# A third buffer for result tiles behind the y phase, and a later place for layer 1's third unit, in a two-layer graph kernel

## The chip, the cores and the metric

The kernel runs on one core of a Trainium2 chip. The metric is the time of one execution on the device in microseconds (us), and lower is better. The engines of a core work side by side, each through its own list of instructions in order: PE (TensorE, matrix products), DVE (VectorE), ACT (ScalarE), POOL (GpSimd, which here issues nearly all gathers and scatters) and SP (SyncE, which issues the plain transfers). An instruction that waits for another engine or for a transfer holds back everything behind it on its own engine.

## The reference, cut to what matters

A graph of 2708 nodes with 1024 features each, and two layers. Layer 0 is attention over the neighbours of a node, layer 1 a sum over the neighbours. Each is followed by a residual and a layer norm.

```python
# layer 0
q = x @ W_q.T + b_q;  k = x @ W_k.T + b_k;  v = x @ W_v.T + b_v
z = (q @ k.T) / sqrt(1024) * adj
z = where(z == 0, -10000, z)
x = layernorm(x + relu(softmax(z, axis=1) @ v))
# layer 1
x = layernorm(x + adj @ (x @ weight) + bias)
```

The matrix `adj` holds zeros and ones and is nearly empty, so the kernel works with lists of neighbours.

## The kernel before

**Blocks.** The rows are sorted by their number of neighbours and cut into 22 blocks of 128 rows. Block 0 holds the rows with most neighbours, block 21 (the list `last`) is the short one of 20 rows without any. `SLOTS` gives the neighbours that a block can have.

**The stages.** First the weights of q and k are multiplied into one matrix, and the lists of neighbours are made from `adj`. Then the y phase computes a row of scores' factors per row of x (`y_block`, L319 to L328), block by block, and stores it in DRAM. Beside it, and behind it, "jobs" attend: they gather y rows (`yg`) and neighbours' rows (`g`), take scores on DVE (L774), and sum the neighbours' rows with the weights of the softmax into a tile `r` (L831). A finished `r` is transposed by PE (L698) and copied to SBUF by ACT (L699).

**The projections of layer 0.** Until the y phase is over, blocks are projected one at a time: `project` (L721), then `finish0`, which adds the bias into a tile `t` (L867), applies relu and adds the row's own x (L869), normalises with `norm` (ACT at L757 to L770) and scatters the tile `t` to the DRAM tensor of layer 1's inputs (L685, called x_d in the profile). Blocks 1, 0 and 21 come last in this manner. Behind them seven pairs of blocks follow, (7, 20), (19, 18) and so on. A pair is one 2 by 2 block product in seven half products where eight would be the plain way (`pair_products`, products at L958). It needs sums and differences of the two transposed tiles (`turn_pair`, L947 to L950, tile `s_all`), and differences of the weights, made once on DVE (L1089 to L1092; the profile calls these tiles t as well). Between the products DVE adds partial results from PSUM into the two result tiles (`add`, L970), since only four PSUM banks serve the products. `finish_pair` (L1027) does for a pair what `finish0` does for a block.

**Where the result tiles lie.** Tiles named `t` come from two pools. The pool `work` (`wp`) has two buffers of `t`, used in turn: by every block of `finish0` and by the first tile of every pair. The pool `xb` exists only behind the y phase, in memory that the y phase used before; it has two buffers of `t`, for the second tile of every pair. A buffer is free again when the scatter of the tile before has landed. So the first tile of pair (7, 20) takes the buffer of block 0, and the first tile of pair (19, 18) that of block 21.

**Layer 1.** It runs over 11 units of one or two blocks, the first four being (20), (19, 18), (17, 16) and (15, 1). `sum_rows` gathers neighbours' rows on POOL and sums them on DVE (L1189, L1191). `turn1` transposes and takes sums and differences as above. `gather_x1` copies the bias into a tile `xr` on ACT (L1198), and a gather on POOL adds the rows' own x to it. `work1` makes the products, and `finish1` normalises and scatters to the output.

**What sets the order.** A scheduler orders each engine's instructions when the program is built. It goes by the order of the code, by priorities (the adds from PSUM are urgent) and by its own estimates. `follow` adds a dependency by hand; with `same=True` it is between two instructions of one engine and only fixes their order. In layer 1, the sums of the third unit, (17, 16), stand in the code ahead of the loop, thus ahead of the second unit's `turn1` and `gather_x1`.

Of the kernel before, what the change touches and what calls it, by code (L numbers as in the profile page):

```python
# [9 lines left out]
F32 = mybir.dt.float32  # L10
# [5 lines left out]
ALU = mybir.AluOpType  # L16
# [4 lines left out]
P = 128  # L21
# [59 lines left out]
def sparse_part(ctx, tc, x, xT, adj, wqT, wkT, wvT, bq, bk, bv, w1, b1, out):  # L81
    nc = tc.nc
    N, D = x.shape
# [15 lines left out]
    last = [b for b in range(NB) if SLOTS[b] == 0]  # L99
# [12 lines left out]
    with es:  # L112
# [146 lines left out]
        for c in range(DC):  # L259
            nc.vector.scalar_tensor_tensor(junk[:, :D], wq_i[c // 2][:, c % 2, :], scale, bk_bc, op0=ALU.mult,  # L260
                                           op1=ALU.mult, accum_out=u_col[:, c:c + 1])
        for c in range(DC):
            nc.vector.scalar_tensor_tensor(junk[:, D:2 * D], wk_i[:, c, :], 1.0, bq_bc, op0=ALU.mult,
                                           op1=ALU.mult, accum_out=y_col[:, c:c + 1])
        nc.vector.scalar_tensor_tensor(junk[:, :DC], bq_sb, scale, bk_sb, op0=ALU.mult,
                                       op1=ALU.mult, accum_out=bqk)
# [69 lines left out]
        def follow(later, earlier, same=False):  # L336

            kind = mybir.DependencyClass.NoSync if same else mybir.DependencyClass.Sync
            tc.add_manual_dep(later.ins, earlier.ins.name, mybir.DependencyInfo(kind, mybir.DependencyReason.DATA),
                              reason="an engine's queue shall not stand still for a transfer")  # L340
# [287 lines left out]
        for b in range(FAMILY):  # L628
# [8 lines left out]
            elif FAMILY - DC // 2 - 2 <= b < FAMILY - 2:  # L637
                for c in range(2 * (b - FAMILY + DC // 2 + 2), 2 * (b - FAMILY + DC // 2 + 2) + 2):
                    for h in range(NH):
                        put = nc.sync.dma_start(out=wv_q[c // 4][h][:, c % 4, :],  # L640
                                                in_=wvT[c * P:(c + 1) * P, h * HALF:(h + 1) * HALF])
# [14 lines left out]
        wp = es.enter_context(tc.tile_pool(name="work", bufs=2, reuse_waits="tile"))  # L656
# [27 lines left out]
        def scatter(dst, b, n, src, group):  # L684
            put = nc.gpsimd.indirect_dma_start(  # L685
                out=dst, out_offset=bass.IndirectOffsetOnAxis(ap=tabs[:n, b, ROW:ROW + 1], axis=0),
                in_=src[:n], in_offset=None)
            tc.declare_no_dep(put.ins, group=group, reason="disjoint rows: a row's number is in one record")
            tc.add_to_no_dep_group(group, put.ins)
# [59 lines left out]
        def norm(t, sm, n, sm2=None):  # L749

            nm = stat.tile([P, 1], F32, name="lnm")
            if sm2 is None:
                nc.vector.tensor_scalar_mul(nm[:n], sm[:n], -1.0 / D)
            else:
                nc.vector.tensor_scalar(nm[:n], sm[:n], sm2[:n], -1.0 / D, op0=ALU.add, op1=ALU.mult)  # L755
            vs = stat.tile([P, 1], F32, name="vs")
            nc.scalar.activation(junks[:n], t[:n], AF.Square, bias=nm[:n], accum_out=vs[:n])  # L757

            lv = stat.tile([P, 1], F32, name="lv")
            nc.scalar.activation(lv[:n], vs[:n], AF.Ln, bias=eps[:n], scale=1.0 / D)  # L760
            near = stat.tile([P, 1], F32, name="near")
            nc.scalar.activation(near[:n], lv[:n], AF.Exp, scale=-0.5)
            ve = stat.tile([P, 1], F32, name="ve")
            nc.vector.scalar_tensor_tensor(ve[:n], vs[:n], D * EPS, near[:n], op0=ALU.add, op1=ALU.mult)
            nc.vector.tensor_scalar(ve[:n], ve[:n], near[:n], -0.5 / D, op0=ALU.mult, op1=ALU.mult)
            rstd = stat.tile([P, 1], F32, name="rstd")
            nc.vector.scalar_tensor_tensor(rstd[:n], ve[:n], 1.5, near[:n], op0=ALU.add, op1=ALU.mult)
            nmr = stat.tile([P, 1], F32, name="nmr")
            end = nc.vector.tensor_tensor(nmr[:n], nm[:n], rstd[:n], op=ALU.mult)  # L769
            applied.append(nc.scalar.activation(t[:n], t[:n], AF.Identity, bias=nmr[:n], scale=rstd[:n]))  # L770
            return end
# [88 lines left out]

        def finish0(b, po, xr):
            n = rows[b]
            t = wp.tile([P, D], F32, name="t")
            for h in range(NH):
                hs = slice(h * HALF, (h + 1) * HALF)
                with tc.high_priority(URGENT):
                    nc.vector.tensor_add(t[:n, hs], po[h][:n], bias_bc[:n, hs])  # L867
            sm = stat.tile([P, 1], F32, name="sm")
            nc.vector.scalar_tensor_tensor(t[:n], t[:n], 0.0, xr[:n], op0=ALU.max, op1=ALU.add, accum_out=sm[:n])  # L869
            end = norm(t, sm, n)  # L870
            scatter(x1_d[:, :], b, n, t, "x1")
            return end
# [60 lines left out]
            yield  # L933


        def turn_pair(flips, pool):

            A = []
            for k, flip_to in enumerate(flips):
                rT = (pool if k else wp).tile([P, DC, P], F32, name="rT", bufs=2)  # L940
                A.append(flip_to(rT))
            if len(flips) == 1:
                return A, None
            (a11, a12), (a21, a22) = [(a[:, :DC // 2], a[:, DC // 2:]) for a in A]
            s_all = wm_pool.tile([P, 4, DC // 2, P], F32, name="s_all", tag="m3")
            S = [s_all[:, i] for i in range(4)]
            nc.vector.tensor_add(S[0], a21, a22)  # L947
            nc.vector.tensor_sub(S[1], S[0], a11)
            nc.vector.tensor_sub(S[2], a11, a21)
            nc.vector.tensor_sub(S[3], a12, S[1])  # L950
            return A, S

        def differences():
# [8 lines left out]
        def halves_of(t):  # L962
            return t[:, :HALF], t[:, HALF:]
# [4 lines left out]
        def add(to, acc, what):  # L968
            with tc.high_priority(URGENT):
                nc.vector.tensor_add(to, acc, what)  # L970
# [39 lines left out]
            return a[:, :DC // 2], a[:, DC // 2:]  # L1010

        def project_pair(pair, A, S):
            ts = [(xb_pools[0] if k else wp).tile([P, D], F32, name="t", bufs=2) for k in range(2)]
            bias = halves_of(bias_bc)

            def whole(k, h, acc, what):
                add(halves_of(ts[k])[h], acc, what)

            pair_products(A, S, wv_q, wv_t, [bias, bias], [halves_of(t) for t in ts], whole, pair == pairs[-1])
            return ts  # L1020
# [13 lines left out]
        got, xb_bc, xb_pools, pair_x = {}, [], [], {}  # L1034
# [137 lines left out]
        units = [(20,), (19, 18), (17, 16), (15, 1), (14, 2), (7, 8), (9, 3), (4, 10), (6, 0), (5, 11), (12, 13)]  # L1172
        assert sorted(last + [b for unit in units for b in unit]) == list(range(NB))
        last_norm = applied[-1]
        firsts = []

        def sum_rows(b, k=0):
            if b == "hub":
                n, tab, ok, r = P, tab_h, valid_h, part
            else:  # L1180
                n, tab, ok = (P, tab0, valid0) if b == 0 else (rows[b], tabs[:, b, :SLOTS[b]], valid[:, b, :SLOTS[b]])
                r = (cp if k else wp).tile([P, D], F32, name="r", bufs=RB)
            for j in range(tab.shape[1] if b else J0):
                if j == 0 and b not in [0, "hub"] + single + MIXED:
                    gather_slot(x1_d[:, :], tab[:n, 0:1], n, r)
                    continue
                xg = gather_slot(x1_d[:, :], tab[:n, j:j + 1], n, g_tile())
                if j == 0:
                    firsts.append(nc.vector.tensor_scalar(r[:n], xg[:n], ok[:n, 0:1], None, op0=ALU.mult))  # L1189
                else:  # L1190
                    nc.vector.scalar_tensor_tensor(r[:n], xg[:n], ok[:n, j:j + 1], r[:n], op0=ALU.mult, op1=ALU.add)  # L1191
            return r

        def gather_x1(b, k=0):

            n = rows[b]
            xr = (cp if k else wp).tile([P, D], F32, name="xr", bufs=2 if k else 3)
            follow(nc.scalar.copy(xr[:n], bias1[:n]), last_norm, same=True)  # L1198
            return gather_at(x1_d[:, :], tabs[:n, b, ROW:ROW + 1], n, xr, ALU.add)
# [40 lines left out]
        got1, turned1, pending = {}, {}, []  # L1240
# [5 lines left out]
        nc.vector.tensor_sub(t3, t2, w11)  # L1246
        nc.vector.tensor_sub(t4, w21, t2)
        xrs = {0: [gather_x1(b, k) for k, b in enumerate(units[0])]}
        got1[2] = [sum_rows(b, k) for k, b in enumerate(units[2])]
        for i, unit in enumerate(units):  # L1250
            for p in pending:
                finish1(*p)
            if i + 1 < len(units):
                turned1[i + 1] = turn1(units[i + 1], got1.pop(i + 1))
                xrs[i + 1] = [gather_x1(b, k) for k, b in enumerate(units[i + 1])]
            if i + 3 < len(units):
                got1[i + 3] = [sum_rows(b, k) for k, b in enumerate(units[i + 3])]
            if i == 4:
                sum_rows("hub")
            pending = list(zip(unit, *work1(unit, *turned1.pop(i), xrs.pop(i))))  # L1260
            if i == 2:
                for b in last:
                    pending.append((b, gather_x1(b), None))
# [319 lines left out]
```

## Time and profile before

| | |
|---|---|
| median of three runs | 1090.86 us (1090.35 to 1092.21) |
| span of the profiled execution | 1091.0 us |
| busy: PE, DVE, ACT, POOL | 1015.2, 826.3, 428.1, 486.7 us |
| PE's products of pairs and units (L958, three groups) | 126.6 + 87.9 + 72.1 us |
| mean granted clock of PE | 0.976 |

The span has four parts for the reader of this case: up to about 540 us the weights, the lists and the y phase; from 540 to 582 the last single blocks 1, 0 and 21; from 582 to 771 the seven pairs; and from 783 to the end layer 1. Between 770.7 and 783.1 PE has nothing to do, since layer 1 gathers rows that layer 0 has to write first. The names in the profile are those of the program without their numbers: `t<-po,bias_bc` at L970 is an `add` into a result tile, `x_d<-t,tabs` at L685 is a scatter of a result tile, `g<-in_x_dram,tabs` a gather of neighbours' rows in layer 0 and `g<-x_d,tabs` in layer 1.

### The profile page before, as it was taken

The numbers are of one execution on the slowest core, as the hardware profiler recorded it, in microseconds if no ns is written. First come the engines' busy times: TensorE is split into PE (matmuls) and PEld (weight loads), VectorE is DVE, ScalarE is ACT, GpSimd is POOL, SyncE is SP. The second block draws the span as 40 slices with busy tenths as digits, with TensorE's granted clock in tenths as the row PEclk, the third lists the DMA queues.
The fourth block names the chain that finished last, engine by engine and source line by source line (L and its number), as shares of the span: only waits on it lengthen the run. The fifth ranks groups of instructions, "written<-read, shape, count | busy, mean of one in ns | idle before, by whom it ended". The sixth has DMA issues, their size and how long they took to land.

```text
span 1091.0 us, 10751 instructions
## 1 busy us (share of the span) xinstructions
PE 1015.2 (93%) x3177; PEld 540.1 (50%) x3177; DVE 826.3 (76%) x1801; ACT 428.1 (39%) x896; POOL 486.7 (45%) x397
## 2 busy tenths in 40 slices
PE   7999999999798989999998999999589999999993
PEld 6444466556454545466644444444244444445441
DVE  8799999980487789965297999984477777896431
ACT  4688697412131323232333253342512363324322
POOL 1000230067453546623066476631477777887300
PEclk9999999999999999999999899999799999999997
DMA  9555468435786746635142487835598689979601
GB/s 363 193 211 202 164 219 292 137 95 153 259 261 209 236 160 222 212 126 187 43 124 97 140 275 261 280 125 183 159 302 245 207 241 320 297 221 321 180 39 41
DMA packets 85219, 218.22 MB, mean 200 GB/s; under 512 B 15354, under 2 KB 37338, under 8 KB 82444
## 3 DMA queue, kind: packets, MB, share of 16 engines
q0 software_dynamic: 48768, 148.05, 42.3%
q1 hardware_dynamic: 36384, 69.40, 18.8%
q8 instruction: 27, 0.44, 0.2%
q14 instruction: 40, 0.33, 0.1%
HBM read 208.60 MB, written 33.68 MB: 222 GB/s over the span
## 4 chain that ended last, share of the span: by engine, by line
DVE 32%; PE 28%; issue 18%; DMA 10%; POOL 7%; ACT 3%; POOLq 0%; DVEq 0%; ACTq 0%
PE po L958 17%; PE po L319 6%; DVE few L225 6%; DVE a L222 5%; DVE junkv L774 5%; DMA g<-in_x_dram,tabs 4%; DVE r L831 3%; PE po L721 2%; POOL g L349 2%; DVE t L970 1%; POOL tab_d L563 1%; DMA g<-x_d,tabs 1%; DMA yg<-y_d,tabs 1%; PE tr L247 1%; POOL xr L343 1%
## 5 line engine op out<-in xcount | busy, mean ns | idle before, releaser
L319 PE MATMUL po<-m_sb,xt 128*128 128x343 f32 (+1 forms) x1008 | 296.3, 454 | 11.5 <-DVE yo L323 6.3
L319 PEld LDWEIGHTS po<-m_sb,xt 128*128 128x128 f32 x1008 | 190.4, 190 | 111.9 <-DVE yo L323 8.0
L774 DVE SCALAR_TENSOR_TENSOR junkv<-yg,g 128x1024 uint8<-128x1024 f32 x109 | 133.1, 1221 | 28.5 <-DMA g<-in_x_dram,tabs 16.2
L349 POOL DMA_INDIRECT g<-in_x_dram,tabs x86 | 114.3, 1330 | 76.4 <-ACT r L829 25.2
L958 PE MATMUL po<-t,s_all 128*128 128x512 f32 x272 | 126.6, 609 | 10.6 <-DVE t L970 6.5
L1191 DVE SCALAR_TENSOR_TENSOR r<-g,valid,r 128x1024 f32<-128x1024 f32 x77 | 98.6, 1281 | 17.8 <-DMA g<-x_d,tabs 17.2
L608 PE MATMUL po<-wk_o,wq_o 128*128 128x512 f32 x256 | 110.5, 592 | 0.0
L721 PE MATMUL po<-wv,rT 128*128 128x512 f32 x224 | 101.7, 611 | 6.2 <-DVE yo L323 2.8
L757 ACT ACTIVATE junks<-t,lnm 128x1024 uint8<-128x1024 f32 (+1 forms) x43 | 49.3, 1147 | 120.8 <-DVE lnm L755 103.9
L332 ACT ACTIVATE junka<-xt 128x128 f32<-128x128 f32 x176 | 53.9, 307 | 100.7 <-PE po L319 62.1
L958 PEld LDWEIGHTS po<-t,s_all 128*128 128x128 f32 x272 | 52.6, 196 | 78.2 <-issue 61.1
L958 PE MATMUL po<-w,rT 128*128 128x512 f32 x192 | 87.9, 607 | 0.0
L349 POOL DMA_INDIRECT g<-x_d,tabs x67 | 77.0, 1149 | 22.7 <-issue 16.5
L831 DVE SCALAR_TENSOR_TENSOR r<-g,pr,r 128x1024 f32<-128x1024 f32 x64 | 82.0, 1281 | 6.3 <-ACT r L843 4.8
L563 POOL DMA_INDIRECT tab_d<-rec,pos_i x22 | 25.1, 1141 | 129.9 <-DVE pos_i L552 123.5
L770 ACT ACTIVATE t<-t,nmr,rstd 128x1024 f32<-128x1024 f32 (+1 forms) x43 | 52.5, 1237 | 70.7 <-DVE nmr L769 64.2
L225 DVE MAX8 few<-a 128x8 f32<-128x75 f32 (+3 forms) x132 | 78.8, 616 | 0.0
L608 PEld LDWEIGHTS po<-wk_o,wq_o 128*128 128x128 f32 x256 | 48.4, 190 | 59.3 <-issue 59.0
L721 PEld LDWEIGHTS po<-wv,rT 128*128 128x128 f32 x224 | 43.2, 195 | 60.0 <-issue 53.5
L958 PE MATMUL po<-w,s_all 128*128 128x512 f32 x160 | 72.1, 592 | 0.0
L222 DVE SCALAR_TENSOR_TENSOR a<-a,iota 128x2708 f32<-128x2708 f32 (+1 forms) x22 | 65.2, 2963 | 5.4 <-ACT junk L221 5.4
L220 ACT ACTIVATE junk<-a 128x2708 uint8<-128x2708 f32 (+1 forms) x22 | 54.1, 2458 | 26.9 <-DMA a<-in_adj_dram 22.3
(332 smaller groups left out, 1475.4 us busy)
## 6 DMA issues: line engine op xcount, KB each, us to landing
a<-in_adj_dram SPq DMA_DIRECT2D x21, 1354.0 KB, 5.7
y_d<-yo SPq DMA_DIRECT2D x21, 514.0 KB, 5.4
xt<-in_xT_dram SPq DMA_DIRECT2D x21, 512.0 KB, 5.6
wq_i<-in_wqT_dram SPq DMA_DIRECT2D x8, 512.0 KB, 10.0
wk_i<-in_wkT_dram SPq DMA_DIRECT2D x8, 512.0 KB, 10.2
wv<-in_wvT_dram SPq DMA_DIRECT2D x16, 256.0 KB, 6.8
w<-in_w_dram SPq DMA_DIRECT2D x4, 1024.0 KB, 6.5
g<-in_x_dram,tabs POOLq DMA_INDIRECT x86, 5.6
```

What stands on the lines that cost most here:

```text
L220: nc.scalar.activation(junk[:n], a[:n], AF.Sign, accum_out=cnt[:n, b:b + 1])
L222: nc.vector.scalar_tensor_tensor(a[:n], a[:n], 1.0, iota[:n], op0=ALU.is_equal, op1=ALU.mult)
L225: nc.vector.max(few[:n, i * 8:(i + 1) * 8], a[:n, cuts[i]:cuts[i + 1]])
L319: put = nc.tensor.matmul(po[:, :k1 - k0], xt[:, c, :], m_sb[c // 2][:, c % 2, k0:k1], start=(c == 0), stop=(c == DC - 1))
L332: put = nc.scalar.activation(junka, xts[b][:, c, :], AF.Copy, accum_out=xs[:, c, b:b + 1])
L349: nc.gpsimd.indirect_dma_start(out=dst[:n], out_offset=None, in_=src, in_offset=bass.IndirectOffsetOnAxis(ap=at, axis=0), bounds_check=N - ...
L608: nc.tensor.matmul(po, wq_o[i // 2][:, o, i % 2 * P:(i % 2 + 1) * P], wk_o[:, o, hs], start=(o == 0), stop=(o == DC - 1))
L721: put = nc.tensor.matmul(acc, rT[:, c, :], w[c // 4][h][:, c % 4, :], start=(c == 0), stop=(c == DC - 1))
L774: nc.vector.scalar_tensor_tensor(junkv[:n], yg[:n, :D], scale, xg[:n], op0=ALU.mult, op1=ALU.mult, accum_out=s)
L831: nc.vector.scalar_tensor_tensor(r[:n], xg[j][:n], pr[:n, j:j + 1], r[:n], op0=ALU.mult, op1=ALU.add)
L958: put = nc.tensor.matmul(acc, a[:, k], w[:, k], start=start and k == 0, stop=stop and k == DC // 2 - 1, skip_group_check=True)
L1191: nc.vector.scalar_tensor_tensor(r[:n], xg[:n], ok[:n, j:j + 1], r[:n], op0=ALU.mult, op1=ALU.add)
```

## The change

It has two parts. In the first, the result tiles of blocks 0 and 21 (`[0] + last`) come from the pool `xb`, whose `t` gets a third buffer. The pool `work` keeps two, so that the first tile of pair (7, 20) takes the buffer of block 2 or 1, which are further back. In the second, the sums of layer 1's third unit move in the code behind the second unit's `turn1` and `gather_x1`, and the first sum of each of its two blocks is ordered on DVE behind the last difference of the second unit (`halves_turned[-1]`).

```diff
         def finish0(b, po, xr):
             n = rows[b]
-            t = wp.tile([P, D], F32, name="t")
+            t = xb_pools[0].tile([P, D], F32, name="t", bufs=3) if b in [0] + last else wp.tile([P, D], F32, name="t")
...
         def turn_pair(flips, pool):
...
-            nc.vector.tensor_sub(S[3], a12, S[1])
+            halves_turned.append(nc.vector.tensor_sub(S[3], a12, S[1]))
...
         def project_pair(pair, A, S):
-            ts = [(xb_pools[0] if k else wp).tile([P, D], F32, name="t", bufs=2) for k in range(2)]
+            ts = [(xb_pools[0] if k else wp).tile([P, D], F32, name="t", bufs=2 + k) for k in range(2)]
...
-        def sum_rows(b, k=0):
+        def sum_rows(b, k=0, behind=None):
...
+                if behind is not None:
+                    follow(put, behind, same=True)
+                    behind = None
...
-        got1[2] = [sum_rows(b, k) for k, b in enumerate(units[2])]
         for i, unit in enumerate(units):
...
             if i + 1 < len(units):
                 turned1[i + 1] = turn1(units[i + 1], got1.pop(i + 1))
                 xrs[i + 1] = [gather_x1(b, k) for k, b in enumerate(units[i + 1])]
+            if i == 0:
+                got1[2] = [sum_rows(b, k, halves_turned[-1]) for k, b in enumerate(units[2])]
```

In the built program PE, ACT and SP issue what they issued before; PE's and ACT's order differs by neighbours that change places in layer 0. On DVE the adds of pair (7, 20) stand earlier, and the rest of layer 0 differs by small swaps; in layer 1 two sums of the third unit stand behind the four differences of the second. On POOL one gather of y rows late in layer 0 stands behind two gathers of `xr`, and in layer 1 the two `xr` gathers of the second unit stand ahead of the third unit's four gathers.

More of the change, by code (lines that the diff above doesn't have):

```diff
@@ L933, in attend_shares @@
             yield
+        halves_turned = []
         def turn_pair(flips, pool):
@@ L1188, in sum_rows @@
                 if j == 0:
-                    firsts.append(nc.vector.tensor_scalar(r[:n], xg[:n], ok[:n, 0:1], None, op0=ALU.mult))
-                else:
-                    nc.vector.scalar_tensor_tensor(r[:n], xg[:n], ok[:n, j:j + 1], r[:n], op0=ALU.mult, op1=ALU.add)
+                    put = nc.vector.tensor_scalar(r[:n], xg[:n], ok[:n, 0:1], None, op0=ALU.mult)
+                    firsts.append(put)
+                else:
+                    put = nc.vector.scalar_tensor_tensor(r[:n], xg[:n], ok[:n, j:j + 1], r[:n], op0=ALU.mult, op1=ALU.add)
+                if behind is not None:
+                    follow(put, behind, same=True)
+                    behind = None
             return r
```

## The prediction

> **What bounds the kernel now.** I read first the busy times of each engine in stretches that I cut at the idle times of PE (columns: stretch, its length, busy time of PE, PE weight loads, DVE, ACT and POOL with instruction counts, granted PE clock, DMA share, GB/s):
>
> ```profile
> 581.50:594.80 13.30, 13.25 (x38) 5.94 (x36) 12.21 (x20) 6.69 (x13) 11.77 (x2) 1.00 0.13 40
> 594.80:601.30 6.50, 0.04 (x1) 0.04 (x1) 0.79 (x2) 0.00 (x0) 2.94 (x3) 0.84 0.48 162
> 601.30:619.20 17.90, 17.90 (x42) 8.30 (x43) 16.56 (x38) 4.43 (x9) 8.83 (x7) 0.87 0.50 152
> 619.20:649.00 29.80, 29.80 (x83) 14.01 (x81) 29.65 (x63) 11.62 (x21) 20.40 (x15) 1.00 0.74 239
> 649.00:735.00 86.00, 84.89 (x240) 40.29 (x239) 82.46 (x202) 38.26 (x72) 47.61 (x39) 1.00 0.65 222
> 735.00:770.70 35.70, 35.68 (x85) 15.78 (x83) 15.60 (x43) 8.35 (x15) 3.58 (x4) 1.00 0.56 193
> ```
>
> PE runs without a stop to 594.8, stands 6.5 us, and then runs almost without a stop to 770.7. DVE stands in the same hole and is then as full as PE until about 730; after that it has room. So before the hole, inside it and after it nothing but this one stop is loose. The timeline of PE and of DVE at that place (start, length, instruction, idle time before it and what ended it), and POOL's:
>
> ```profile
> 592.87 1.88 PE L958 MATMUL po<-wv,rT 128*128 128x512 f32 x4
> 601.26 6.07 PE L958 MATMUL po<-t,s_all 128*128 128x512 f32 x8 [6.51 <-DVE t L970]
> 608.89 3.60 PE L958 MATMUL po<-t,s_all 128*128 128x512 f32 x8
> ```
>
> ```profile
> 592.44 1.26 DVE L831 SCALAR_TENSOR_TENSOR r<-g,pr,r 128x1024 f32<-128x1024 f32 x1
> 600.51 1.29 DVE L970 TENSOR_TENSOR t<-po,bias_bc 128x512 f32<-128x512 f32 x2 [6.81 <-DMA x_d<-t,tabs]
> 607.37 0.69 DVE L970 TENSOR_TENSOR t<-po,bias_bc 128x512 f32<-128x512 f32 x1 [1.07 <-PE po L958]
> ```
>
> ```profile
> 587.11 7.48 POOL L349 DMA_INDIRECT g<-in_x_dram,tabs  x1 [0.30 <-DVE rstd L767]
> 594.89 0.93 POOL L343 DMA_INDIRECT xr<-in_x_dram,tabs  x1 [0.30 <-issue]
> 596.13 1.00 POOL L685 DMA_INDIRECT x_d<-t,tabs  x1 [0.30 <-issue]
> ```
>
> The chain reads from the right: PE waits for a DVE add (the first of pair (7, 20)); DVE waits for the scatter of block 0's result, because the add writes the buffer of "t" that this scatter still reads; the scatter stands on POOL behind a gather that took 7.48 us. The result itself was ready at 589.25 (ACT's L770 began at 588.01 and took 1.24).
>
> The second place is the start of layer 1, PE and then DVE:
>
> ```profile
> 802.47 1.99 PE L698 MATMUL tr<-ident,r 128*128 128x128 f32 x16
> 804.29 7.03 PE L958 MATMUL po<-w,rT 128*128 128x512 f32 x16
> 814.87 5.09 PE L958 MATMUL po<-t,s_all 128*128 128x512 f32 x8 [3.54 <-DVE xr L970]
> ```
>
> ```profile
> 801.55 0.68 DVE L1222 SCALAR_TENSOR_TENSOR t<-po,xr 128x512 f32<-128x512 f32 x1
> 807.48 1.28 DVE L1191 SCALAR_TENSOR_TENSOR r<-g,valid,r 128x1024 f32<-128x1024 f32 x1 [5.24 <-DMA g<-x_d,tabs]
> 814.13 0.68 DVE L970 TENSOR_TENSOR xr<-po,xr 128x512 f32<-128x512 f32 x1
> ```
>
> PE stands 3.54 us for the add at 814.13, which DVE reaches only after sums that wait for the fourth unit's gathers.
>
> **What the Trainium skill says.** "TensorE: Matmul & The Clock Gate", section "What's actually happening": an idle window of about 3.4 us halves the clock until a busy window has passed. The trace agrees: the eight matmuls after the hole took 6.07, the same eight later 3.60. "SBUF — State Buffer", section "Who interferes with whom": a DVE instruction with two SBUF inputs blocks a GpSimd instruction that reads SBUF, for its whole length. The trace fits: the 7.48 us gather lay beside the two 2.27 us differences of weights (L1091, L1092), while the gathers of 560 to 625 have a median of 1.22. "Advanced Engine Details and Errata", section "Sequencer Loop": an instruction waits in its engine's queue until its semaphore is ready. Here DVE issues nothing for 6.81 us, so all behind the add waits too.
>
> **The change part by part.** *The tile of blocks 0 and 21.* Their "t" moves to the pool xb, and xb's "t" gets three buffers. In the built program the first add of pair (7, 20) waits for PE alone, and stands ahead of L1091 on DVE; the second add of the pair now stands between the two differences.
>
> - On PE: 6.51 of idle time goes, and 6.07 - 3.60 = 2.47 of half clock: 9.0 us.
> - On DVE: 6.81 goes, and the waits for the slow matmuls, 1.07 at 607.37 and 0.23 at 612.52: 8.1 us.
> - I walked the pair with these durations. Products 2 to 5 of 3.44 us each would run from 589.4 to 606.6, and DVE reaches the adds between them 0.5 to 2 us before PE needs them. So no new stop on PE there.
> - From 619 both engines are full (29.80 and 29.65 of 29.80). What PE wins beyond DVE, it gives back in waits for DVE: the smaller number, 8.1, goes through.
>
> *The new buffers' own waits.* Block 0's first add (567.45) and block 21's (580.43) now wait for the stores of y rows that used that memory; POOL's gather at 545.18 had already waited for those. Pair (19, 18) now waits for the scatters of blocks 1 and 0, issued at 572.02 and 596.13 and some 4.3 us in flight, for adds that stand at 620.26 and 627.91 (8 us earlier after the change). Both cost nothing. The third buffer also lifts waits of later pairs that show no idle time: nothing.
>
> *A gather that moves on POOL.* In the changed order the y rows gathered at 693.78 come behind two gathers of xr, of which the second waits for a DVE step that ends at 704.34 and ran 704.61 to 706.30. The y gather would start at 706.6, take about 1.4, and land 3.4 later (as the one issued at 683.64 for 1.59, awaited until 688.64): 711.4. Its first reader stands at 709.83 on DVE. The releasing DVE step is one 0.6 us add earlier in the new order: a loss of 1.0 us on a DVE that has no room. Bounds: 0 to 2. The other swaps on DVE exchange neighbours of 0.1 to 1.3 us: nothing.
>
> *Layer 1.* On DVE two sums (L1191, blocks 17 and 16) move behind four differences (L947 to L950). The differences end some 3 us earlier, but they ended at 801.63 while PE was still with the first unit until 802.47: no gain. On POOL two gathers of xr for blocks 19 and 18 pass four gathers for 17 and 16; the eight together lie where they lay, so everything from 798.87 on keeps its place. The last gather for block 16 ends about 798.5 in place of 793.93, so it lands near 802.4 (it landed 3.9 after its end), the sum ends at 803.6, and PE wants it at about 803.4. That delay disappears in the 3.54 us before 814.87, since the add at 814.13 hangs on other gathers. I take 0. Bounds: a landing of 8.6 us (the longest from 560 to 625) would make PE 4.9 late, of which 3.54 is hidden: a loss of 1.4; a gain up to 1, from xr rows that are there earlier. More is excluded, because DVE's order from 801.55 on is unchanged.
>
> Sum: 8.1 - 1.0 + 0 = 7.1 us. The profiled span is 1091.0, inside the three runs (1090.35 to 1092.21), so I take it off their median: 1090.86 - 7.1 = **1083.8**. The last stretch, 735 to the end, is passed on shifted.
>
> **The rivals.**
>
> *The whole of PE's gain arrives.* The y gather is hidden and PE's lead of 0.9 over DVE is not given back, because PE's three short stops of 0.20, 0.74 and 0.17 after 649 need not grow: 9.0 us, 1081.9. For it: DVE has room from 730. Against: DVE at 29.65 of 29.80.
>
> *The gather takes the place of the scatter (the other side).* The gather of 587.11 ended 0.9 us after DVE fell idle at 593.70. If it ended because DVE stood, it will not end while DVE works on. DVE then arrives at the reader of these rows (score L774, 611.06 before, some 8 us earlier now: 603.0) and stops there. The gather ends at 603.9, and lands 4.6 later (median of that stretch) at 608.5: 5.5 lost. The next gather, behind xr and the scatter, issues by 607.7 and lands at 612.3, where its reader comes at 610.6: 1.7 more. In all 7.1 - 7.2 = -0.1: 1091.0, no change. With landings of 8.6 it is 11.2 lost: 1095.0, slower. It turns slower once the stop is above 7.1 us. For it: the coincidence of the ends. Against: from 619 to 649 DVE was 99% busy and POOL issued 15 operations in 20.40 us; and in the new order two adds that read PSUM lie between and behind the long differences.
>
> *A part of it.* The same gather comes late by 2 to 4 us only, or layer 1 loses its 1.4: 1085.5 to 1088.
>
> That the change doesn't lift the wait is excluded by the built program's waits.
>
> **How the numbers follow.** My forecast (1082.5 to 1085.5) 0.53, the whole gain 0.18, a part 0.16, no change 0.07, slower 0.06. A difference of 0.2% (2.2 us) is about what can be told from none. Faster: 0.53 + 0.18 + 0.16 = 0.87; same 0.07; slower 0.06. The range goes from 1.4 below the whole gain to the end of the partial case, 1080.5 to 1088.0, and leaves out the last two cases and a little at each side.
>
> **What would show it.** Right: no wait of L970 for the scatter near 594; the first t products at full clock, 0.43 us each; PE idle below 1 us from 582 to 619; PE ending layer 0 near 763.5; a DVE wait for yg of about 1 us near 702; the stop before layer 1's second unit unchanged near 3.5 us. Wrong: DVE waiting for g at about 603, POOL gathers longer than 7.5 us, or a longer stop of PE at the third unit's transposes.

## The result, and the profile after

| | us, median | lowest to highest | profiled span | granted clock |
|---|---|---|---|---|
| before | 1091.53 (4 runs) | 1090.35 to 1093.06 | 1091.0 | 0.976 |
| after | 1084.14 (4 runs) | 1082.77 to 1087.1 | 1083.5 | 0.981 |

The ratio of after to before is 0.9935, with a 95% interval from 0.9908 to 0.9962: 7 us, 4 to 10. The forecast was 1083.8.

Behind L935, lines of the changed kernel lie two to seven lower in its file: L958 is now L960, L970 is L972, L1091 and L1092 are L1093 and L1094, L1191 is L1194.

Busy times by stretches after, the first two cut at the same times as before, the third 8 us earlier (columns as there):

```profile
581.50:594.80 13.30, 13.30 (x38) 6.26 (x37) 13.30 (x22) 5.11 (x11) 11.72 (x5) 1.00 0.26 74
594.80:601.30 6.50, 6.50 (x16) 2.85 (x16) 6.50 (x15) 2.39 (x4) 5.35 (x4) 1.00 0.64 195
641.00:727.00 86.00, 83.45 (x229) 38.66 (x228) 80.23 (x193) 36.19 (x67) 46.06 (x37) 1.00 0.65 220
```

Where PE had 0.04 us of work in 6.50, it now has 6.50. In the third stretch PE is no longer as full as it was (84.89 of 86.00 before, 83.45 now): here it gives something back. PE's timeline at the place of the hole, and then DVE's and POOL's:

```profile
587.31 3.60 PE L960 MATMUL po<-t,s_all 128*128 128x512 f32 x8
```

```profile
584.50 0.68 DVE L972 TENSOR_TENSOR t<-po,bias_bc 128x512 f32<-128x512 f32 x1
```

```profile
586.65 5.68 POOL L343 DMA_INDIRECT xr<-in_x_dram,tabs  x1 [0.67 <-DVE nmr L769]
592.64 1.62 POOL L685 DMA_INDIRECT x_d<-t,tabs  x1 [0.30 <-issue]
```

The pair's first add stands at 584.50 without a wait, none of the pair's adds waits for a scatter, and eight matmuls take 3.60, where the first eight had taken 6.07. POOL is still slow at this place: the scatter of block 0 goes out only at 592.64, behind an instruction of 5.68 us. But nobody waits for it now.

The waits of PE in the pairs, from 579.4 to 761.6 (what waited, for what, us in total, times, longest):

```profile
PE tr L698 <- DVE r L831: 2.1, 4, 1.3
PE tr L698 <- DVE nms L801: 0.5, 1, 0.5
```

Before, PE's waits behind the hole were 0.9 for DVE and 0.2 for ACT. And PE at the start of layer 1:

```profile
796.73 1.06 PE L698 MATMUL tr<-ident,r 128*128 128x128 f32 x8 [1.62 <-DVE r L1194]
806.77 5.40 PE L960 MATMUL po<-t,s_all 128*128 128x512 f32 x8 [2.11 <-DVE xr L972]
816.42 3.70 PE L960 MATMUL po<-t,s_all 128*128 128x512 f32 x8 [0.82 <-DVE xr L972]
```

The one stop of 3.54 us has become three, 4.55 in all.

**Stretch by stretch.** The spans alone mislead, since the part ahead of the pairs ends at other times from run to run. So I cut each profiled execution at the same PE instructions: the first six products of pair (7, 20) (`po<-wv,rT x6`, 581.55 before), the matmul of the flag that ends layer 0 (770.40), the transposes of block 20 that begin layer 1 (783.14), and those of the fourth unit, blocks 15 and 1 (833.53).

| run | first products at | to the flag | block 20 to fourth unit | fourth unit to the end |
|---|---|---|---|---|
| before | 581.55 | 188.85 | 50.39 | 257.47 |
| after | 579.42 | 182.19 | 52.51 | 256.67 |
| difference | -2.13 | -6.66 | +2.12 | -0.80 |

From the flag to block 20 it is 12.7 us in both. The pairs gave 6.66. The 2.13 ahead of them doesn't come from the change: it is there already at a transpose of the y phase (L916, 480.49 before and 478.34 after), far ahead of every tile that the change touches, and from that transpose to the first products it is 101.06 and 101.08. Whether the 2.12 in layer 1 comes from the change, one pair of traces doesn't tell. The experiments have to.

### The profile page after: what moved, and what is told of

Read it like the earlier page. It is cut to its first block, busy times and chain, and to the rows that moved or that the text cites. A ratio compares the mean times of both kernels' runs of the same rounds, so it can differ in the third digit from the quotient of the medians.

```text
span 1083.5 us, 10745 instructions
## 1 busy us (share of the span) xinstructions
PE 1013.6 (94%) x3177; PEld 539.2 (50%) x3177; DVE 827.0 (76%) x1801; ACT 427.9 (39%) x896; POOL 492.7 (45%) x397
## 4 chain that ended last, share of the span: by engine, by line
DVE 33%; PE 29%; issue 16%; DMA 11%; POOL 6%; ACT 3%; POOLq 0%; DVEq 0%; ACTq 0%
PE po L960 17%; PE po L319 6%; DVE few L225 6%; DVE a L222 5%; DVE junkv L774 5%; DVE r L831 4%; DMA g<-in_x_dram,tabs 3%; PE po L721 2%; POOL g L349 2%; DMA g<-x_d,tabs 2%; DMA yg<-y_d,tabs 2%; DVE t L972 1%; POOL tab_d L563 1%; PE tr L247 1%; PE tr L698 1%
## 5 line engine op out<-in xcount | busy, mean ns | idle before, releaser
L349 POOL DMA_INDIRECT g<-in_x_dram,tabs x86 | 110.8, 1288 | 70.9 <-ACT r L829 23.4
L960 PE MATMUL po<-t,s_all 128*128 128x512 f32 x272 | 124.6, 601 | 3.0 <-DVE xr L972 2.9
L1194 DVE SCALAR_TENSOR_TENSOR r<-g,valid,r 128x1024 f32<-128x1024 f32 x77 | 98.6, 1281 | 22.0 <-DMA g<-x_d,tabs 21.4
L721 PE MATMUL po<-wv,rT 128*128 128x512 f32 x224 | 98.3, 595 | 4.7 <-DVE nm L892 2.2
L349 POOL DMA_INDIRECT g<-x_d,tabs x67 | 79.6, 1188 | 22.7 <-issue 14.0
L960 PE MATMUL po<-w,rT 128*128 128x512 f32 x192 | 88.1, 609 | 0.0
L960 PEld LDWEIGHTS po<-t,s_all 128*128 128x128 f32 x272 | 51.8, 192 | 69.5 <-issue 61.1
L960 PE MATMUL po<-w,s_all 128*128 128x512 f32 x160 | 72.1, 592 | 0.0
```

What stands on the lines that cost most here:

```text
L349: nc.gpsimd.indirect_dma_start(out=dst[:n], out_offset=None, in_=src, in_offset=bass.IndirectOffsetOnAxis(ap=at, axis=0), bounds_check=N - ...
L721: put = nc.tensor.matmul(acc, rT[:, c, :], w[c // 4][h][:, c % 4, :], start=(c == 0), stop=(c == DC - 1))
L960: put = nc.tensor.matmul(acc, a[:, k], w[:, k], start=start and k == 0, stop=stop and k == DC // 2 - 1, skip_group_check=True)
L1194: put = nc.vector.scalar_tensor_tensor(r[:n], xg[:n], ok[:n, j:j + 1], r[:n], op0=ALU.mult, op1=ALU.add)
```

## The experiments

The theory, A: the whole gain is the wait of one add for block 0's scatter, lifted in layer 0; the edit of layer 1 brings nothing. Against it: B, the edit of layer 1 brings a part; C, it takes both tiles or the third buffer. Of why the scatter was late there were two opinions: D, a POOL instruction stands still while DVE works on operands in SBUF; E, that one gather is slow for a reason of its own. Of layer 1's start there were two more: F, only DVE's order makes PE stop there; G, the gathers set the pace. The runs came in three groups, each on another chip and beside its own runs of the kernel before, whose median was 1093.05 in the first, 1104.59 in the second and 1104.88 in the third. So only ratios, and stretches between two instructions, are compared across groups.

### The change again, and its two parts alone (first group)

> The change as it is, once more, beside the kernel before on one chip. Theory A (the whole gain is the buffer wait lifted in layer 0; the edit of layer 1 brings nothing or loses a little): 7 us under the kernel before, 0.9935 of it. The profile: no idle time of DVE for the scatter near 594, PE stopped for about 1.6 us for a sum of block 16 near 796 and for about 2.1 us before the second unit of layer 1. Rival B (the edit of layer 1 brings part of it) expects the same here.

Each part alone, as it differs from the kernel before (the first whole, of the second the move only):

```diff
 # first part alone
+            t = xb_pools[0].tile([P, D], F32, name="t", bufs=3) if b in [0] + last else wp.tile([P, D], F32, name="t")
...
+            ts = [(xb_pools[0] if k else wp).tile([P, D], F32, name="t", bufs=2 + k) for k in range(2)]
 # second part alone
-        got1[2] = [sum_rows(b, k) for k, b in enumerate(units[2])]
...
+            if i == 0:
+                got1[2] = [sum_rows(b, k, halves_turned[-1]) for k, b in enumerate(units[2])]
```

> Only the first part: the tiles of blocks 0 and 21 in the pool xb, three buffers there; layer 1 as before. Theory A: all of the gain, 7 us under the kernel before, and 0 to 1.5 us under the whole change, because the stop of 1.6 us for a sum near 796 goes and the old one of 3.5 us before the second unit comes back. Rival B: only a part of the gain, 4 to 5 us, so the whole change is faster than this one by over 2 us.

> Only the second part: two sums of layer 1 (blocks 17 and 16) held behind the last of the four differences of weights, and with it two gathers of xr ahead of four gathers of g on POOL; tiles and buffers as before. Theory A: between the kernel before and 1.5 us over it; the hole of 6.5 us in PE near 595 is there. Rival B: 2 us or more under the kernel before.

Measured: the whole change 0.9923 (0.9904 to 0.9943), the first part alone 0.9937 (0.9919 to 0.9956), the second part alone 0.9994 (0.9982 to 1.0005). The second part's own PE timeline has the hole of before, and both new stops of layer 1:

```profile
599.52 5.46 PE L960 MATMUL po<-t,s_all 128*128 128x512 f32 x8 [6.64 <-DVE t L972]
802.95 1.06 PE L698 MATMUL tr<-ident,r 128*128 128x128 f32 x8 [1.54 <-DVE r L1194]
813.59 5.40 PE L960 MATMUL po<-t,s_all 128*128 128x512 f32 x8 [2.71 <-DVE xr L972]
```

and the first part's has one long stop in layer 1:

```profile
806.34 6.34 PE L958 MATMUL po<-t,s_all 128*128 128x512 f32 x8 [4.84 <-DVE xr L970]
```

A holds, and alone the second part brings nothing: it is the kernel before, within 0.2%. It cuts one stop in two, and doesn't shorten it. Beside the first part, the whole change is 0.0014 lower than the first part alone, some 1.5 us with intervals that overlap. So B's 2 us and more isn't seen, but a smaller share of the second part, when both stand together, is not excluded here; the last table bears on it.

### One tile of the two, without a third buffer (first and second group)

```diff
-            t = wp.tile([P, D], F32, name="t")
+            t = xb_pools[0].tile([P, D], F32, name="t", bufs=2) if b in [0] else wp.tile([P, D], F32, name="t")
```

and the same with `if b in last` (block 21) in place of `if b in [0]`.

> Of the first part only the tile of block 0 is taken from xb, with two buffers there as before: no third buffer, block 21's tile where it was, layer 1 as before. Theory A with one wait as the whole cause (the add of pair (7, 20) waits for block 0's scatter, since it writes the buffer that this scatter reads): the same time as with the first part whole, 7 us under the kernel before, because the add now takes block 1's buffer, whose scatter was issued at 572. Rival C (it takes both tiles, or the third buffer, since without it a later pair waits in the same way): at most half of that, 0 to 4 us under the kernel before, with a new idle time of DVE at L970 for a scatter between 607 and 650.

> The other half of the first part: only the tile of block 21 is taken from xb, with two buffers there as before; block 0's tile is where it was. Theory A: the same time as with block 0's tile alone, 6 to 7 us under the kernel before, because either of the two tiles leaves the buffer of block 1 to the first add of pair (7, 20). Rival C (block 0's tile has to go): no gain, 0 to 1 us, with the wait of DVE for block 0's scatter as before.

Block 0's tile alone: 0.9938 (0.9916 to 0.9959). Block 21's alone: 0.9945 (0.9927 to 0.9963). From the first products to the flag they took 182.07 and 182.10, the first part whole 181.79, the change 182.19. PE with block 21's tile alone, the first product that waited before:

```profile
598.05 3.60 PE L958 MATMUL po<-t,s_all 128*128 128x512 f32 x8
```

C falls: either tile, with two buffers, is worth as much as both with three. It is enough that one of the last two tiles before the pairs, block 0's or block 21's, leaves that pool, because the first add then falls on the buffer of block 1, whose scatter was out long before (issued at 572.02 in the trace of before). To move block 1's own tile would not do: the two buffers would then turn over blocks 0 and 21, and the first add would fall on block 0's again. That follows from the turn of the buffers and was not run.

### Block 0's scatter ahead of the gather (second group)

```diff
+        def behind_scatter(put):
+            if ahead:
+                seen.append(put)
+                if len(seen) in (13, 25):
+                    follow(put, ahead[0], same=True)
...
+            if b == 0:
+                ahead.append(put)
```

`behind_scatter` is called for each gather that is written behind the scatter; the 13th is the one of 7.48 us, the 25th that of xr behind it. The order on PE, DVE and ACT is that of before.

> The kernel before with its own tiles and buffers; only POOL's order differs: block 0's scatter goes ahead of the gather of g that took 7.48 us and of one gather of xr. Theory D (a POOL gather or scatter stands still while DVE works on instructions with two inputs in SBUF): the scatter starts at about 589.3 beside the differences L1091 and L1092 and the sum behind them, so it is long itself and ends when these end, near 594.6 in place of 597.1; the wait of DVE for it shrinks from 6.8 to about 4.3, and the time is some 2.5 us under the kernel before. Rival E (that one gather is long for a reason of its own, and the scatter only had the bad place behind it): the scatter takes 1 us, lands near 594.5, DVE waits less than 1.5 us, and the time is about 6 us under the kernel before.

Measured: 0.9962 (0.9948 to 0.9977), 4.2 us. POOL, DVE and PE at the place (L695 is the scatter, L983 the add, L971 the product):

```profile
598.58 5.05 POOL L695 DMA_INDIRECT x_d<-t,tabs  x1 [2.73 <-ACT t L781]
603.94 1.02 POOL L358 DMA_INDIRECT g<-in_x_dram,tabs  x1 [0.30 <-issue]
```

```profile
601.49 1.26 DVE L842 SCALAR_TENSOR_TENSOR r<-g,pr,r 128x1024 f32<-128x1024 f32 x1
606.10 1.29 DVE L983 TENSOR_TENSOR t<-po,bias_bc 128x512 f32<-128x512 f32 x2 [3.35 <-DMA x_d<-t,tabs]
```

```profile
606.85 3.70 PE L971 MATMUL po<-t,s_all 128*128 128x512 f32 x8 [3.05 <-DVE t L983]
```

Now the scatter takes 5.05 us, and the gather that had taken 7.48 takes 1.02, so the slowness belongs to the place and not to that gather. E falls. As in the kernel before, the slow POOL instruction ends just behind DVE's work: here 0.88 after the sum (601.49 + 1.26 = 602.75, and 598.58 + 5.05 = 603.63), before 0.89 (593.70 and 594.59), after the change 0.81 (L1094 ended at 591.52, the gather at 592.33). That is a coincidence of three places and no rule: the gather of xr ahead of them, 4.29 us in the traces of before and after, ended only 0.10 after DVE's L950 (586.80 and 586.70 before), while DVE's next work in SBUF was under way. D said 5.3 us for the scatter, and a wait of 4.3; the wait was 3.35, because the scatter was awaited for 2.47 after its end and not 3.4. The gain is larger than the 2.5 that I had said: the shorter stop didn't halve the clock (3.70 for the first eight, 6.07 before). From the first products to the flag it was 183.41, 5.4 less than before. This run also bears on a rival that has no letter. In the kernels with a moved tile the scheduler puts the pair's adds and products into another order, too; here the order on PE, DVE and ACT is the old one, and a shorter wait alone brings 5.4 us with 3.05 of PE's stop still there. So the gain doesn't need the new order; what the order adds by itself was not separated.

### What a gather costs beside DVE's work (second and third group)

Behind the last step of the kernel before, groups of gathers were put beside one kind of DVE work each.

```diff
+            [lambda: nc.vector.tensor_sub(flat[0], flat[1], flat[2])] * 8,          # both inputs in SBUF
+            [lambda: nc.vector.scalar_tensor_tensor(...)] * 14,                      # the sums' form
+            [lambda: nc.vector.tensor_add(flat[0][:, :HALF], acc, flat[1][:, :HALF])] * 26,   # acc in PSUM
+            [lambda: nc.vector.tensor_copy(flat[0], flat[1])] * 15,
```

> The kernel before, and behind its last step five groups of four gathers of 128 rows of 1024 on POOL, each group beside one kind of work on DVE: nothing; eight differences of 2048 with both inputs in SBUF; fourteen sums of 1024 (scalar_tensor_tensor) with both tensors in SBUF; 26 adds of 512 with one input in PSUM and one in SBUF; fifteen copies of 2048 from SBUF. The time of the whole is not compared. Theory D: about 1.0 us for a gather beside nothing and beside the adds from PSUM; beside the differences and beside the sums the first gather lasts until DVE is nearly done with its group (over 10 us). Rival E: 1.0 to 2.0 us for each of them beside every kind of work.

POOL's timeline: a gather with no such work beside it, one beside the differences, one beside the sums, one beside the adds from PSUM, one beside the copies:

```profile
1092.96 1.03 POOL L349 DMA_INDIRECT g<-x_d,tabs  x1 [0.83 <-DVE g L1281]
1106.55 3.36 POOL L349 DMA_INDIRECT g<-x_d,tabs  x1 [0.30 <-issue]
1130.02 2.30 POOL L349 DMA_INDIRECT g<-x_d,tabs  x1 [0.30 <-issue]
1153.32 0.99 POOL L349 DMA_INDIRECT g<-x_d,tabs  x1 [0.30 <-issue]
1177.03 2.82 POOL L349 DMA_INDIRECT g<-x_d,tabs  x1 [0.31 <-issue]
```

Neither expectation was met whole: the work in SBUF slows a gather, the adds from PSUM don't, but none was held for 10 us. The DVE instructions of this kernel each waited for the one before, so I mended D: perhaps a gather slips in at DVE's pauses. The second version gives DVE five outputs in turn, so that it need not pause:

```diff
+            [lambda k=k: nc.vector.tensor_sub(outs[k], left, right) for k in range(5)],   # without a wait
+            [lambda k=k: nc.vector.tensor_sub(outs[0], left, right) for k in range(5)],   # each waits for the last
```

> The kernel before, and behind its last step five groups of three gathers of 128 rows of 1024 on POOL, each of which starts when the first DVE instruction of its group has ended: five differences of 2048 with both inputs in SBUF into five different tiles, so that DVE goes from one to the next without a wait; the same five into one tile, each waiting for the one before; nine sums of 1024 without a wait between them; eighteen adds of 512 from PSUM without a wait; five copies of 2048 without a wait. The time of the whole is not compared. Theory D, mended (a gather stands still while DVE goes from one instruction with SBUF inputs to the next without a gap, and gets its 0.8 us when DVE pauses): beside the first group and beside the sums the first gather lasts until DVE is done, 8 to 10 us; beside the second group 2 to 3.5 us; beside the adds from PSUM 1.0 us; beside the copies not said. Rival E (no gather is held for longer than one DVE instruction): at most 3.5 us beside each group, the first like the second.

POOL (two gathers beside the first group, then the first one beside each of the other four), and the last four of DVE's first five differences:

```profile
1094.92 2.83 POOL L349 DMA_INDIRECT g<-x_d,tabs  x1 [5.13 <-DVE t L1280]
1098.06 1.88 POOL L349 DMA_INDIRECT g<-x_d,tabs  x1 [0.30 <-issue]
1112.30 2.92 POOL L349 DMA_INDIRECT g<-x_d,tabs  x1 [10.19 <-DVE t L1281]
1128.67 1.78 POOL L349 DMA_INDIRECT g<-x_d,tabs  x1 [8.80 <-DVE t L1282]
1142.60 0.99 POOL L349 DMA_INDIRECT g<-x_d,tabs  x1 [8.52 <-DVE t L1284]
1157.62 2.12 POOL L349 DMA_INDIRECT g<-x_d,tabs  x1 [11.45 <-DVE t L1285]
```

```profile
1094.57 8.88 DVE L1280 TENSOR_TENSOR w<-t,t 128x2048 f32<-128x2048 f32 x4
```

The mended D falls and E's bound stands: 2.83 without pauses, 2.92 with them. The four differences from 1094.57 take 2.22 each, so one ends near 1096.8 and the next near 1099.0; the gathers end at 1097.75 and 1099.94, 0.9 after each. Beside the differences a gather looks as if it waited for the one DVE instruction under way and then took its own 0.9. By that rule the scatter of the last experiment, begun at 598.58, would have ended near 600.1 and not at 603.63. So two things are shown: the place beside DVE's work in SBUF makes POOL slow, and plain streams of that work cost a gather at most 3.4 us. What makes it 5 to 7.5 in the kernel (the mixture with instructions of one column, or the other engines at work, which the groups lack) stays open.

### The add ahead in layer 1 (second and third group)

Both kernels, before and after, stop before the second unit because DVE reaches the add behind sums that wait for gathers. I tried to lift that in place of the change's second part:

```diff
...
+        def first_product(A, w, base, to):
+            pa = bank()
+            half_products(pa, halves_of_turned(A[0])[0], w[0][0], stop=False)
+            return pa, add(to[0][0], pa, base[0][0])
...
+            if i == 0:                           # i < 2 in the version for two units
...
+                early[1], put = first_product(turned1[1][0], w1_q, xs_, xs_)
+                got1[3] = [sum_rows(b, k, put) for k, b in enumerate(units[3])]
```

> The first part of the change alone, and in layer 1 another order in place of the change's second part: the first product of the second unit is put ahead of the third unit's transposes on PE, and the sums of block 15 behind the add that reads this product on DVE. Theory F (the stop of 3.5 to 4.8 us before the second unit is only DVE's order: the add is ready some 8 us before DVE reaches it, behind sums that wait for the fourth unit's gathers): the stop is gone, with 1.5 to 2.7 us of half clock after it, and the time is 5 to 7 us under the first part alone, 11 to 13 under the kernel before. Rival G (the gathers of the fourth unit bound layer 1's start, and the stop only moves to the fourth unit's transposes near 820): less than 2 us under the first part alone.

> The kernel with one add ahead once more, on the same chip as the whole change: both theories expect 1 to 3 us under the whole change, with PE's first stops in layer 1 shorter by some 4 us in all and 1 to 3 us of new ones in the third unit.

> As the kernel with the add ahead (first part of the change; first product of the second unit of layer 1 ahead of the third unit's transposes, sums of the fourth unit behind its add), and the same once more for the third unit: its first product ahead of the fourth unit's transposes, the sums of the fifth unit behind the add that reads it. Theory F (DVE's order alone makes these stops): the stops of 1.80 and 1.16 us that PE had in the third unit near 846 and 861 go too, and the time is 2 to 4 us under the kernel with one add ahead and 3 to 6 us under the whole change. Rival G (the gathers set the pace of layer 1's start): the stops move on to the fifth unit, and the time is that of the kernel with one add ahead, within 1 us.

> The whole change once more, to be compared on this chip with the two kernels beside it: 0.992 to 0.995 of the kernel before.

Measured in the second group: 0.9932 (0.9908 to 0.9955) with one add ahead. In the third: 0.9912 (0.9879 to 0.9944) with one, 0.9931 (0.9906 to 0.9955) with two, and the whole change 0.9936 (0.9911 to 0.9961). PE with one add ahead (second group), and with two:

```profile
823.74 3.70 PE L958 MATMUL po<-t,s_all 128*128 128x512 f32 x8 [1.45 <-DVE xr L970]
845.74 3.70 PE L958 MATMUL po<-t,s_all 128*128 128x512 f32 x8 [1.80 <-DVE xr L970]
860.90 3.70 PE L958 MATMUL po<-t,rT 128*128 128x512 f32 x8 [1.16 <-DVE t L1231]
```

```profile
861.14 6.48 PE L958 MATMUL po<-t,rT 128*128 128x512 f32 x8 [4.31 <-DVE t L1231]
```

F is right about the place: the stop before the second unit is gone (the first wait of PE there is now the 1.45 ahead of its third product from s_all). It is wrong about its worth: smaller stops come in the third unit, and with two adds ahead one of 4.31 with half a clock behind it. That is G, in its result. Its cause is not shown: ahead of the stop of 4.31 DVE waits 6.40 us for gathered rows, until 857.86, but the step that PE needs (L1231) again stands on DVE behind the sums of these rows. So the gathers come late, as G has it, and DVE's order turns this into a stop of PE, as F has it; which of the two a further change would have to lift was not tested. No version here is shown to beat the change: the best is 0.9912 against 0.9936, with intervals that overlap.

### All the stretches

Each profiled execution, cut as above; the last column is the whole of layer 1, from block 20's transposes to the end (span less their start; before: 1091.0 - 783.14).

| run | first products at | to the flag | layer 1 |
|---|---|---|---|
| before | 581.55 | 188.85 | 307.9 |
| second part alone | 579.67 | 188.36 | 307.7 |
| scatter ahead | 590.59 | 183.41 | 307.8 |
| first part alone | 578.38 | 181.79 | 308.3 |
| block 0's tile alone | 584.91 | 182.07 | 307.5 |
| block 21's tile alone | 590.16 | 182.10 | 310.0 |
| after, three times | 579.42, 580.57, 591.19 | 182.19, 182.17, 181.73 | 309.2, 306.2, 309.2 |
| one add ahead, twice | 592.81, 592.85 | 181.75, 181.86 | 307.8, 307.4 |
| two adds ahead | 591.83 | 182.29 | 309.5 |

The second column has two values, 188.6 and 182.0, and one between them for the scatter ahead: all of the gain that is seen lies here. Layer 1 has no such steps. With the edit of layer 1 (after three times, second part alone) its mean is 308.1, without it (before, first part, either tile, scatter ahead) 308.3, and three runs of one kernel, the change, differ by up to 3. An effect of the second part of less than some 2 us, either way, could hide in that.

## Why the prediction was right, point by point

**The tile: right in its mechanism, 6.6 in place of 7.1 us.** PE's stop of 6.51 and the half clock are gone, the pair's products run on without a stop as walked, and either tile alone does the same. (The walk's "products 2 to 5" are five, the last five of the pair's seven: 5 times 3.44 is the 17.2 from 589.4 to 606.6. After the change they ran from 587.31 to 604.48, 17.2.) The sum as predicted was DVE's 8.1 less 1.0 for the gather of y. Measured from the first products to the flag: 188.85 - 182.19 = 6.66. PE's idle time in it fell from 7.62 to 2.76, which is 4.86 and not 6.5, because PE's short waits grew from 1.1 to 2.6: the step "what PE wins beyond DVE, it gives back" fits, and the rival with the whole gain of PE, 9.0, is out. PE's busy time fell by 1.80 (181.23 to 179.43), where the half clock alone was 2.47; where the other 0.67 went I can't say from these traces.

**The new buffers' own waits: nothing, right.** No add of a pair waits for a scatter, with three buffers or with two.

**The gather of y that moves: 1.0 us, right in its size, in part by luck.** DVE waited 0.3 for yg in the pairs of before. After:

```profile
DVE junkv L774 <- DMA yg<-y_d,tabs: 1.3, 2, 0.9
```

The wait of 0.9 is the one that was forecast. But the gather ended at 696.24 and DVE waited for it until 700.82: 4.6 in flight, where I had put 3.4. It also began 4.8 us ahead of DVE's need (695.08, for 699.88), where I had put 3.8 (706.6, for 709.83, less the add of 0.6). The two errors cancel.

**Layer 1: zero was right, two of its steps were not.** "PE wants it at about 803.4", and the sum ends at 803.6, was a delay of 0.2; it measured 1.62, and 1.60, 1.54 and 1.87 in the other three runs with the edit. The last gather for block 16 ended at 790.70 and DVE waited for it until 795.29: 4.6 in flight, where I had put 3.9. And the gathers did not lie where they had lain: the last one ended some 1.0 later than the prediction has it (798.5, less the 8.82 by which block 20's transposes came earlier, is 789.7). A longer stop at the third unit's transposes stood among the prediction's own signs of being wrong. It came, and the runs show no loss from it. And the stop before the second unit did not stay near 3.5: it was 2.11, 1.54, 2.71 and 1.54 with the edit. What I had argued, that the delay disappears in that stop, agrees with the sums, within their spread. The stops of PE between the third unit's transposes and the fourth's sum to 4.55, 3.65, 4.25 and 3.90 with the edit, and to 3.54, 4.84, 4.58, 4.33 and 4.56 in the five kernels without it (means 4.1 and 4.4).

**The total: 1084.14, forecast 1083.8.** The three ratios of the whole change, 0.9935, 0.9923 and 0.9936, would bring the 1090.86 to between 1082.5 and 1083.9. PE ended layer 0 at 761.61 where I had named 763.5, but it had begun the pairs 2.13 earlier. The two profiled spans differ by 7.5, and of that agreement with 7.1 a part is luck: the 2.13 of an earlier start and the 2.12 lost in layer 1 nearly cancel, the first doesn't come from the change and the second isn't shown to (the three traces of the change differ by 3 in layer 1 alone).

**The gather in the scatter's place: didn't happen.** After the change the slow POOL instruction is a gather of xr that nobody awaits soon, and it took 5.68, not the 16 or more that this rival needed. DVE stood for no gather of g near 603. The rival had rested on the gather ending because DVE fell idle. Here POOL's instruction ended at 592.33, with DVE at work without a pause: after L1094, at 591.52, it had an add from PSUM, and from 592.11 again a sum in SBUF. So it does not take an idle DVE to end it. Whether the add from PSUM let it through, as the prediction had said against this rival, is argued and not shown.

**The slow gather.** For it I had leaned on the Trainium skill, "SBUF — State Buffer", section "Who interferes with whom": a DVE instruction with two SBUF inputs contends with a GpSimd instruction that reads SBUF. I had left out that the same section reports a probe in which DVE's tensor_tensor, unlike its tensor_copy, did not stall transfers that GpSimd issues. The groups of gathers show that it does here: 1.9 to 3.4 us beside the differences, which are tensor_tensor with both inputs in SBUF, against 0.99 beside adds from PSUM. The 5 to 7.5 us in the kernel are more than that section and these groups explain.

**The half clock behind a stop.** The Trainium skill, "TensorE: Matmul & The Clock Gate", section "What's actually happening", has an idle window of about 3.4 us halving the clock. The stops of 6.51 before the change and 3.05 with the scatter ahead agree (6.07 and 3.70 for the first eight matmuls); the stops of 2.11 and 2.71 in layer 1 don't, as told below, and there the measurement decides.

## What to carry to other kernels

A buffer that a late scatter still reads holds up the engine that writes it next, and through that engine everything behind it (here DVE for 6.81 us and PE for 6.51). Look for the tiles worked last before a change of stage; where their pool has two buffers, it was enough here to give one of the last two tiles another pool. Where two engines are both full behind the stop, forecast the smaller of their two gains, less what moves on the queues beside them: in this one case 8.1 (DVE) and not 9.0 (PE), less 1.0, with 6.66 measured. Cut both traces at the same instructions before believing a difference of spans: here the part ahead of the change moved by more than 2 us without any edit that acts there, and layer 1 by 3 between runs of one kernel.

## What was not expected of the hardware

- A stop's length alone doesn't tell whether the clock is halved behind it. First eight matmuls after stops of PE: 5.40 us after 2.11 (after the change, 806.77) and after 2.71 (second part alone), but 3.70 after 3.05 (scatter ahead) and after 2.88 (one add ahead, third group). Behind stops of 3.54 and more the first eight were slow each time, in the pairs and in layer 1: 5.09 after 3.54, 6.48 after 4.31, 6.34 after 4.84. Why some shorter stops do it and longer ones don't stays open.
- Copies of 2048 with one input in SBUF slow a gather too, to 2.82 and 2.12 us; adds of 512 with an input in PSUM do not, 0.99.
- Whichever instruction of POOL stood beside DVE's work ahead of pair (7, 20) took 5 to 7.5 us (the gather of g 7.48, that of xr 5.68, the scatter 5.05), and the one behind it 0.9 to 1.6. The cause is open.
